# Late field pairs and seven weight tiles loaded in two parts: 112 rows in 14 groups from GpSimd's queue, 16 rows from ScalarE's

## The chip, the cores and the metric

The kernel runs on one core of a Trainium2 chip. The metric is the time of one execution in device microseconds. Before the change it is 756.43 us, the median of 4 runs (756.16 to 756.96).

The engines in what follows: PE (TensorE), DVE (VectorE), ACT (ScalarE), POOL (GpSimd) and SP (SyncE). Transfers between HBM and the on-chip memory are issued by an engine's queue and carried by 16 DMA engines.

## The reference: products of field pairs

For a batch of 1024, 32 fields of 128 numbers, and one 128 x 128 weight matrix for each of the 496 pairs of fields i < j:

```python
v_i = inputs[:, I_IDX, :]
v_j = inputs[:, J_IDX, :]
transformed = jnp.einsum('bpd,ped->bpe', v_i, W)
return transformed * v_j
```

All in float32. The output, 1024 x 496 x 128 numbers, is 260 MB; the inputs are 16.8 MB of fields and 32.5 MB of weights.

## The kernel before

**Data.** The host hands over the fields as `xt[d, field, batch]` and the weights as `wt[c, d, pair, e]`, eight pairs to a tile `c`, in the order of the work. On the chip d, later e, lies on the 128 partitions. One field is a tile of 128 x 1024 (512 KB, 4 KB in a row), a weight tile 128 x 8 x 128 (also 512 KB), an output buffer `ot` 128 x 4 x 1024 (2 MB: four pairs).

**Order.** `_pairs` (L31) lists the pairs with i from 30 down to 0 and j from i + 1 to 31. The main loop (L195) steps through u = 2 x pair + half; a half is 512 of the batch. The order of instructions is that of the program text (`manual_schedule`, L157), so each engine works through its list as written. `first(u)` (L161) starts a half, `second(u)` (L174) ends it three steps later (LAG).

**Work of a half.** The first 15 pairs use float32 matmuls (L168). All later ones split both sides in a high and a low part and use three fast matmuls: two at L171, ACT scales the sum in place (L172), a third is added at L180. DVE multiplies with field j into `ot` (L186). Then SP sends the buffer off, one transfer of 2 MB per four pairs (L193). The pool `o` has three buffers (L68): the fourth group can't be written before the first has gone out.

**Splits.** `split_w` (L95) makes the three parts of two pairs' weights: one instruction on ACT (L100), three on POOL (L101 to L103). `split_x` (L109) does it for half a field: ACT L115, POOL L116 and L117, and the third part on POOL (L121) or, for the first fields, on DVE (L214). The list `todo` (L129) holds them by the pair that needs them; the loop takes at most one of them per pair (L208 to L212), a weight chunk from five pairs ahead of its use on.

**Loads.** The first fields and weight tiles are loaded at the start. After that `load_x` (L73) loads field i - 7 at the first pair of row i (L199), and `load_w` (L88) loads weight tile c into one of three buffers (WB) at the pair that `w_at` (L148) names. Both are issued from ACT's queue, 128 rows at a time. Field 0 comes last, into a weight buffer (L204). POOL issues no transfer.

Of the kernel before, what the change touches and what calls it, by code (L numbers as in the profile page):

```python
# [7 lines left out]
F32 = mybir.dt.float32  # L8
# [3 lines left out]
P = 128  # L12
NF = 32
NQ = NF * (NF - 1) // 2
BT = 1024
HB = 512
WC = 2
WL = 8
# [7 lines left out]
WLEAD = 12  # L26
XAFTER = 54
XLEAD = 5


def _pairs():  # L31
# [5 lines left out]
def kernel(  # L37
# [22 lines left out]
    nc = tc.nc  # L60
# [3 lines left out]
    xpool = ctx.enter_context(tc.tile_pool(name="x", bufs=1))  # L64
# [6 lines left out]
    x_sb = {}  # L71

    def load_x(f, n=1, pieces=1, eng=None):  # L73

        if f == 0:

            t = rpool.tile([P, WL, P], F32, tag="w", name="x_0").rearrange("p q e -> p (q e)").unsqueeze(1)
        else:
            t = xpool.tile([P, n, BT], F32, tag=f"x{f}", name=f"x_{f}")
        s = BT // pieces  # L80
        for k in range(pieces):
            (eng or nc.sync).dma_start(out=t[:, :, k * s : (k + 1) * s], in_=xt[:, f : f + n, k * s : (k + 1) * s])
        for k in range(n):
            x_sb[f + k] = t[:, k, :]

    w_raw = {}

    def load_w(c, splits=(0, WL), eng=nc.scalar):  # L88
        w_raw[c] = rpool.tile([P, WL, P], F32, tag="w", name=f"w_{c}")
        for a, b in zip(splits, splits[1:]):  # L90
            eng.dma_start(out=w_raw[c][:, a:b, :], in_=wt[c, :, a:b, :])

# [30 lines left out]
    nq0 = NATIVE * (NATIVE + 1) // 2  # L123
# [11 lines left out]
    todo.sort(key=lambda t: t[1])  # L135

    load_w(0, (0, 1, WL), nc.sync)
    load_x(NF - 2, pieces=2, eng=nc.scalar)
    load_x(NF - 1, pieces=2, eng=nc.scalar)
    load_x(NF - 3)  # L140
    load_x(NF - 4)
    load_w(1, eng=nc.sync)
    for f in range(NF - 5, NF - 4 - XLEAD, -1):
        load_x(f)
    load_w(2, eng=nc.sync)


    w_at = {}  # L148
# [4 lines left out]
    x_at = XAFTER * WL - 11  # L153
    assert x_at not in w_at and len(w_at) == NQ // WL - WB


    ctx.enter_context(tc.manual_schedule())  # L157
    po, ots = {}, {}
# [2 lines left out]
    def first(u):  # L161
        q, h = divmod(u, 2)
        i, c = pairs[q][0], q // WC
        r = slice(q % WC * P, (q % WC + 1) * P)
        s = slice(h * HB, (h + 1) * HB)
        po[u] = ppool.tile([P, HB], F32, tag="po", name=f"po_{u}")
        if q < nq0:
            nc.tensor.matmul(po[u], w_raw[q // WL][:, q % WL, :], x_sb[i][:, s], start=True, stop=True)  # L168
        else:
            for t in (0, 1):  # L170
                nc.tensor.matmul(po[u], w_s[c][t][:, r], x_s[i][t][:, s], start=t == 0, stop=t == 1)  # L171
            nc.scalar.mul(po[u], po[u], 1.0 + EPS)  # L172

    def second(u):  # L174
        q, h = divmod(u, 2)
        i, j = pairs[q]
        r = slice(q % WC * P, (q % WC + 1) * P)
        s = slice(h * HB, (h + 1) * HB)
        if q >= nq0:
            nc.tensor.matmul(  # L180
                po[u], w_s[q // WC][2][:, r], x_s[i][2][:, s], start=False, stop=True, skip_group_check=True
            )
        g, k = divmod(q, OG)
        if k == 0 and h == 0:
            ots[g] = opool.tile([P, OG, BT], F32, tag="ot", name=f"ot_{g}")
        nc.vector.tensor_tensor(ots[g][:, k, s], po.pop(u), x_sb[j][:, s], ALU.mult)  # L186
        if q >= NQ - 2:
            nc.sync.dma_start(out=out[g, :, k, s], in_=ots[g][:, k, s])
        elif g == 0 or q >= NQ - OG:
            if h == 1:  # L190
                nc.sync.dma_start(out=out[g, :, k], in_=ots[g][:, k])
        elif k == OG - 1 and h == 1:
            nc.sync.dma_start(out=out[g], in_=ots[g])  # L193

    for u in range(2 * NQ + LAG):  # L195
        q = u // 2
        if u < 2 * NQ:
            i, j = pairs[q]
            if u % 2 == 0 and j == i + 1 and 0 < i - 2 - XLEAD:  # L199
                load_x(i - 2 - XLEAD, eng=nc.scalar)  # L200
            first(u)
            if u % 2 == 1 and q in w_at:
                load_w(w_at[q])
            if u == 2 * x_at + 1:  # L204
                load_x(0, eng=nc.scalar)
        if u >= LAG:
            second(u - LAG)
        if u % 2 == 1:  # L208
            ready = [t for t in todo if t[0] <= q]
            if ready:  # L210
                ready[0][2](u)
                todo.remove(ready[0])  # L212
        while later and later[0][0] <= u:
            nc.vector.tensor_tensor(*later.pop(0)[1:], ALU.subtract)  # L214
# [28 lines left out]
```

## Time and profile before

| | |
|---|---|
| median of 4 runs | 756.43 us |
| the profiled execution | 756.16 us, its span 754.3 us |
| busy: PE, DVE, ACT, POOL | 706.7, 624.4, 631.3, 596.5 us |
| moved by DMA | 310 MB in 33,039 packets, 411 GB/s over the span |
| read and written in HBM | 49.3 MB and 260.0 MB |
| loads: issue to landing | 10.6 us (weights from ACT), 11.2 us (fields from ACT), medians |

The span is the time from the first to the last instruction. Part 1 of the page gives each engine's busy time, part 2 the same in 40 slices, part 3 the queues (q1 carries SP's transfers, q10 ACT's, the two of kind "instruction" the engines' code), part 4 the chain of waits that ended last, part 5 the costliest groups of instructions, part 6 the transfers with the time from issue to landing. Matmuls overlap on PE, so the mean length of one is not their distance; that is read from the timeline.

### The profile page before, as it was taken

The page shows a single profiled execution, that of the slowest core. Times are in us where ns is not written, and L with a number is a line of the kernel's source. Part 1 is how long each engine was busy: PE and PEld are TensorE (multiplying, and loading weights), DVE is VectorE, ACT ScalarE, POOL GpSimd, SP SyncE. Part 2 cuts the span into 40 slices and gives each one's busy share as a digit, 9 for nine tenths or more (in the row PEclk, how much of TensorE's full clock was granted, in tenths as well). Part 3 has the DMA queues.
Part 4 walks back from the last instruction along what each step waited for, and adds up shares of the span by engine and source line. Part 5 has one row for each costly group of instructions (what it writes and reads, how often), then busy time and mean ns, then how long its engine had stood idle before and what let it go on. Part 6 is the DMA issues. An engine that isn't in the chain of part 4 may idle for free.

```text
span 754.3 us, 11212 instructions
## 1 busy us (share of the span) xinstructions
PE 706.7 (94%) x2946; PEld 548.0 (73%) x2946; DVE 624.4 (83%) x1012; ACT 631.3 (84%) x1256; POOL 596.5 (79%) x863
## 2 busy tenths in 40 slices
PE   7989999999999999999999999999999999999993
PEld 3567777767777777777777778778787777777872
DVE  4889998888787788888788898888888888898884
ACT  1388988888888888898888889898898998888992
POOL 0988999888888987978879697888887878696660
PEclk9999999999999999999999999999999999999997
DMA  9999999999999999999999999999999999999997
GB/s 352 427 425 428 428 424 428 405 421 395 421 426 414 416 413 409 427 391 428 410 408 425 409 404 421 428 409 407 424 406 412 409 407 407 421 381 429 427 416 301
DMA packets 33039, 310.06 MB, mean 411 GB/s; under 512 B 3664, under 2 KB 3792, under 8 KB 17360
## 3 DMA queue, kind: packets, MB, share of 16 engines
q1 hardware_dynamic: 20448, 264.77, 84.1%
q10 hardware_dynamic: 12528, 44.57, 15.3%
q8 instruction: 24, 0.39, 0.2%
q14 instruction: 39, 0.32, 0.1%
HBM read 49.28 MB, written 260.05 MB: 410 GB/s over the span
## 4 chain that ended last, share of the span: by engine, by line
DMA 43%; PE 28%; DVE 20%; POOL 5%; issue 2%; ACT 0%; DVEq 0%; ACTq 0%; SPq 0%; POOLq 0%
DMA out_dram<-ot 41%; DVE ot L186 19%; PE po L171 19%; PE po L180 9%; DMA x<-in_xt_dram 2%; POOL xl L116 2%; POOL xd L121 1%; DVE xd L214 1%; POOL xl L117 1%; POOL wl L101 1%; POOL wd L103 0%; POOL wd L102 0%; ACT xh L115 0%; DVEq L186 0%; ACT po L172 0%
## 5 line engine op out<-in xcount | busy, mean ns | idle before, releaser
L186 DVE TENSOR_TENSOR ot<-po,x 128x512 f32<-128x512 f32 x992 | 611.1, 683 | 115.2 <-DMA out_dram<-ot 51.4
L172 ACT ACTIVATE po<-po 128x512 f32<-128x512 f32 x962 | 547.5, 584 | 88.0 <-PE po L171 42.8
L171 PE MATMUL po<-xh,wh 128*128 128x512 f32 x962 | 382.1, 397 | 18.5 <-DVE ot L186 17.4
L171 PE MATMUL po<-xl,wl 128*128 128x512 f32 x962 | 377.2, 392 | 9.2 <-POOL wl L101 9.0
L180 PE MATMUL po<-xd,wd 128*128 128x512 f32 x962 | 376.4, 392 | 3.2 <-DVE xd L214 2.7
L171 PEld LDWEIGHTS po<-xh,wh 128*128 128x128 f32 x962 | 180.9, 188 | 80.4 <-DVE ot L186 42.8
L101 POOL TENSOR_TENSOR wl<-w,wh 128x256 fp32r<-128x256 f32 x241 | 180.7, 750 | 71.1 <-ACT wh L100 67.6
L171 PEld LDWEIGHTS po<-xl,wl 128*128 128x128 f32 x962 | 181.0, 188 | 49.2 <-POOL wl L101 14.5
L180 PEld LDWEIGHTS po<-xd,wd 128*128 128x128 f32 x962 | 181.0, 188 | 44.1 <-ACT po L172 4.2
L103 POOL TENSOR_TENSOR wd<-wl,wd 128x256 fp32r<-128x256 f32 x241 | 180.3, 748 | 20.1
L102 POOL TENSOR_SCALAR wd<-wh 128x256 fp32r<-128x256 f32 x241 | 99.5, 413 | 20.3
L100 ACT ACTIVATE wh<-w 128x256 fp32r<-128x256 f32 x241 | 99.5, 413 | 5.6 <-DMA w<-in_wt_dram 4.0
L116 POOL TENSOR_TENSOR xl<-x,xh 128x512 fp32r<-128x512 f32 x52 | 68.8, 1324 | 20.2 <-ACT xh L115 19.8
L121 POOL TENSOR_TENSOR xd<-xh,xl 128x512 fp32r<-128x512 f32 x32 | 41.4, 1292 | 2.7
L115 ACT ACTIVATE xh<-x 128x512 fp32r<-128x512 f32 x52 | 32.6, 631 | 12.3 <-DMA x<-in_xt_dram 12.2
L117 POOL TENSOR_SCALAR xl<-xl 128x512 fp32r<-128x512 f32 x52 | 33.1, 637 | 4.6
L168 PE MATMUL po<-x,w 128*128 128x512 f32 x60 | 28.1, 631 | 4.2 <-DMA x<-in_xt_dram 4.2
L168 PEld LDWEIGHTS po<-x,w 128*128 128x128 f32 x60 | 11.6, 200 | 19.8 <-issue 12.1
L214 DVE TENSOR_TENSOR xd<-xh,xl 128x512 fp32r<-128x512 f32 x20 | 16.1, 807 | 3.9 <-POOL xl L117 3.9
L115 ACT ACT_TABLE_LOAD x1 | 1.3, 1283 | 4.1 <-DMA w<-in_wt_dram 4.1
L230 POOL MEMSET const-float32-0.0<- 128x1 f32 x1 | 0.1, 99 | 0.2 <-issue 0.2
L230 POOL MEMSET const-bfloat16-1.0<- 128x1 bf16 x1 | 0.1, 103 | 0.0
(2 smaller groups left out, 0.2 us busy)
## 6 DMA issues: line engine op xcount, KB each, us to landing
out_dram<-ot SPq DMA_DIRECT2D x122, 2048.0 KB, 12.5
w<-in_wt_dram ACTq DMA_DIRECT2D x59, 512.0 KB, 10.6
x<-in_xt_dram ACTq DMA_DIRECT2D x24, 512.0 KB, 11.2
x<-in_xt_dram SPq DMA_DIRECT2D x6, 512.0 KB, 8.6
out_dram<-ot SPq DMA_DIRECT2D x6, 512.0 KB, 9.9
x<-in_xt_dram ACTq DMA_DIRECT2D x4, 256.0 KB, 5.6
w<-in_wt_dram SPq DMA_DIRECT2D x2, 512.0 KB, 8.2
out_dram<-ot SPq DMA_DIRECT2D x4, 256.0 KB, 8.9
```

Of the source, the lines that this page charges most:

```text
L100: nc.scalar.mul(h, raw, 1.0 - 2.0**-13)
L101: nc.gpsimd.tensor_tensor(l, raw, h.bitcast(F32), ALU.subtract)
L102: nc.gpsimd.tensor_scalar(d, h.bitcast(F32), EPS, 1.0, ALU.mult, ALU.mult)
L103: nc.gpsimd.tensor_tensor(d, l.bitcast(F32), d.bitcast(F32), ALU.subtract)
L116: nc.gpsimd.tensor_tensor(l, x_sb[f][:, s], h.bitcast(F32), ALU.subtract)
L117: nc.gpsimd.tensor_scalar(l, l.bitcast(F32), 1.0 / EPS, 1.0, ALU.mult, ALU.mult)
L121: nc.gpsimd.tensor_tensor(d, h.bitcast(F32), l.bitcast(F32), ALU.subtract)
L168: nc.tensor.matmul(po[u], w_raw[q // WL][:, q % WL, :], x_sb[i][:, s], start=True, stop=True)
L171: nc.tensor.matmul(po[u], w_s[c][t][:, r], x_s[i][t][:, s], start=t == 0, stop=t == 1)
L172: nc.scalar.mul(po[u], po[u], 1.0 + EPS)
L180: nc.tensor.matmul(po[u], w_s[q // WC][2][:, r], x_s[i][2][:, s], start=False, stop=True, skip_group_check=True)
L186: nc.vector.tensor_tensor(ots[g][:, k, s], po.pop(u), x_sb[j][:, s], ALU.mult)
```

## The change

Fields 14 to 1 are loaded in twos, (13, 14) to (1, 2), 8 KB in a row, at the pairs (i, i + 8) for i = 17, 15, ... 5. These seven loads and those of weight tiles 45, 47, 49, 51, 54, 57 and 59 go through `load_apart`: rows 0 to 111 are issued by POOL, rows 112 to 127 by ACT. For the first part the source is written as 14 groups of 8 rows with a step of 14 rows between the rows of a group, and the host puts the rows of these fields and tiles in that order, so that they arrive where they did.

`move_on(k)` issues a transfer of 2 k rows of 64 bytes in k groups from POOL, into a tile that nothing reads: k = 5 at the first split pair, k = 2 three pairs after each load that went apart, k = 13 after the last. 5 + 14 x 14 + 13 x 2 + 13 is 240. The older fields down to 15, field 0 and the other weight tiles are loaded as before. The pairs' order, the splits and the outputs stay as they are, and the instructions other than transfers keep their order on every engine. `dynamic_dma_scratch_size` goes from 256 to 2048.

```diff
--- before.py
+++ after.py
@@ -28,6 +28,18 @@
 XLEAD = 5
 
 
+NE = 14
+ROWS = 8 * NE
+XAPART = 14
+XSTEP, XPOS = 4, 8
+WAPART = (45, 47, 49, 51, 54, 57, 59)
+BACK = 3
 def _pairs():
 
     return [(i, j) for i in range(NF - 2, -1, -1) for j in range(i + 1, NF)]
@@ -85,8 +97,28 @@
 
     w_raw = {}
 
+    mark = xpool.tile([32, 16], F32, tag="mark", name="mark")
+    def move_on(k):
+        nc.gpsimd.dma_start(out=mark[: 2 * k], in_=xt[: 2 * k, 0, :16].rearrange("(b a) n -> a b n", a=k))
+    def load_apart(dst, src):
+        nc.gpsimd.dma_start(out=dst[:ROWS], in_=src[:ROWS].rearrange("(b a) m n -> a b m n", a=NE))
+        nc.scalar.dma_start(out=dst[ROWS:], in_=src[ROWS:])
+    def load_x_apart(f):
+        t = xpool.tile([P, 2, BT], F32, tag=f"x{f}", name=f"x_{f}")
+        load_apart(t, xt[:, f : f + 2, :])
+        for k in range(2):
+            x_sb[f + k] = t[:, k, :]
     def load_w(c, splits=(0, WL), eng=nc.scalar):
         w_raw[c] = rpool.tile([P, WL, P], F32, tag="w", name=f"w_{c}")
+        if c in WAPART:
+            load_apart(w_raw[c], wt[c])
+            return
         for a, b in zip(splits, splits[1:]):
             eng.dma_start(out=w_raw[c][:, a:b, :], in_=wt[c, :, a:b, :])
 
@@ -152,6 +184,9 @@
         w_at[max(c * WL - 3 * WC - 5 - early, free)] = c
     x_at = XAFTER * WL - 11
     assert x_at not in w_at and len(w_at) == NQ // WL - WB
+    w_q = {c: q for q, c in w_at.items()}
+    back = []
 
 
     ctx.enter_context(tc.manual_schedule())
@@ -196,11 +231,21 @@
         q = u // 2
         if u < 2 * NQ:
             i, j = pairs[q]
-            if u % 2 == 0 and j == i + 1 and 0 < i - 2 - XLEAD:
+            if u % 2 == 0 and j == i + 1 and XAPART < i - 2 - XLEAD:
                 load_x(i - 2 - XLEAD, eng=nc.scalar)
             first(u)
+            if u == 2 * nq0:
+                move_on(5)
+            f = i - XSTEP
+            if u % 2 == 0 and 0 < f < XAPART and f % 2 == 1 and j == i + XPOS:
+                load_x_apart(f)
+                back.append(q + BACK)
             if u % 2 == 1 and q in w_at:
                 load_w(w_at[q])
+                if w_at[q] in WAPART:
+                    back.append(q + BACK)
+            if u % 2 == 0 and q in back:
+                move_on(16 - NE if q < w_q[WAPART[-1]] else 13)
             if u == 2 * x_at + 1:
                 load_x(0, eng=nc.scalar)
         if u >= LAG:
@@ -225,9 +270,13 @@
     x = _np.asarray(inputs["r_inputs"])
     w = _np.asarray(inputs["L0_rec_W"])
     xt = _np.ascontiguousarray(x.transpose(2, 1, 0))
+    late = xt[:ROWS, 1 : XAPART + 1].reshape(NE, 8, XAPART, BT)
+    xt[:ROWS, 1 : XAPART + 1] = late.transpose(1, 0, 2, 3).reshape(ROWS, XAPART, BT).copy()
     wt = _np.ascontiguousarray(w[perm].reshape(NQ // WL, WL, P, P).transpose(0, 3, 1, 2))
-
-    nc = _bacc.Bacc("TRN2", target_bir_lowering=False, num_devices=1, dynamic_dma_scratch_size=256)
+    for c in WAPART:
+        wt[c, :ROWS] = wt[c, :ROWS].reshape(NE, 8, WL, P).transpose(1, 0, 2, 3).reshape(ROWS, WL, P).copy()
+    nc = _bacc.Bacc("TRN2", target_bir_lowering=False, num_devices=1, dynamic_dma_scratch_size=2048)
     arrays, args = {}, []
     for name, a in (("xt", xt), ("wt", wt)):
         arrays[f"in_{name}_dram"] = a
```

## The prediction

> **What bounds the kernel now.** I read the page first: part 1 (engines), part 2 (the DMA rows), part 3 (queues), then the chain in one stretch, then the windows.
>
> ```profile
> PE 706.7 (94%) x2946; PEld 548.0 (73%) x2946; DVE 624.4 (83%) x1012; ACT 631.3 (84%) x1256; POOL 596.5 (79%) x863
> ...
> DMA  9999999999999999999999999999999999999997
> ...
> q1 hardware_dynamic: 20448, 264.77, 84.1%
> q10 hardware_dynamic: 12528, 44.57, 15.3%
> q8 instruction: 24, 0.39, 0.2%
> q14 instruction: 39, 0.32, 0.1%
> ...
> out_dram<-ot SPq DMA_DIRECT2D x122, 2048.0 KB, 12.5
> ```
>
> No compute engine is full in every slice, the DMA row is. Parts 3 and 6: 310 MB pass, nearly all of it output, and an output takes 12.5 us to land. The two instruction rows are small as a share of 16 engines, but not as a share of one: q8's 24 packets of 16 KB last 23.8 us in the packet records (0.2% of 16 x 754.3 = 24.1), q14's 39 packets 12.1 us.
>
> The chain between 577 and 604 us shows what DMA holds up:
>
> ```profile
> 566.29 13.23 DMA out_dram<-ot
> ...
> 579.65 4.89 DVE ot L186 x8
> ...
> 584.55 11.65 DMA out_dram<-ot
> ...
> 596.33 4.89 DVE ot L186 x8
> ```
>
> DVE fills an output buffer (4.89 us), the buffer goes out (11.65 to 13.23 us), and DVE may refill it only when its *last* byte is out. With three buffers one such cycle of some 17.6 us carries three groups of four pairs, 5.87 us each. So the slowest part of each transfer counts.
>
> Which part is slow, the landing records tell. Each transfer raises its semaphore 16 times, once per DMA engine. Median us from issue to the 7th, 14th, 15th and 16th of these, over the 2 MB outputs issued in each stretch:
>
> ```
> stretch      7th    14th   15th   16th
> 20 to 60    10.56  11.43  11.68  12.61
> 150 to 250   8.75  10.59  11.57  13.03
> 350 to 450   7.62   8.93  11.42  12.71
> 550 to 650   7.11   8.10   9.51  12.35
> ```
>
> Fourteen engines finish together; one is 2 to 4 us behind them and a second 1 to 2.5. They have the same rows of every transfer as the others, so they do something besides: an extra 24 and 12 us of instruction packets on one engine each would do it (inference: the records name no engine; but no two packets of q8 overlap, as on one engine). Once the lag is as long as the buffers allow, the fourteen idle. The windows show that point:
>
> ```profile
> core 0: us, PE busy (x) PEld busy (x) DVE busy (x) ACT busy (x) POOL busy (x), PEclk, DMA share, GB/s
> 50.00:100.00 50.00, 46.27 (x191) 36.63 (x192) 48.21 (x75) 42.61 (x87) 44.31 (x62) 0.97 1.01 427
> ...
> 150.00:700.00 550.00, 526.75 (x2248) 416.47 (x2247) 460.95 (x752) 487.27 (x971) 453.89 (x662) 1.00 1.00 413
> ```
>
> While the lag builds up: 427 GB/s. After that: 413. If 427 is what the fourteen can do, they lose 550 x (1 - 413/427) = 18.0 us there. Nineteen of q8's packets, 19.2 us, lie in the same stretch: two ways to one size.
>
> **The change, part by part.** The order of all compute instructions on PE, DVE, ACT and POOL stays; only DMA issues move, so the sum has few terms. Profiled execution: 756.16 us (span 754.3 and 1.9 around it), 0.3 below the median 756.43.
>
> *Rows per engine.* Now every load gives each engine 8 of 128 rows. After it, for seven double fields and seven weight tiles, 112 rows go in 14 groups of 8, and 16 rows go one to each of 16 engines. Fourteen engines get 9 rows, two get 1. Packet medians: 4 KB 159 ns, 8 KB 309 ns, 16 KB 611 ns. A double field was 16 x 159 = 2.54 us per engine; it becomes 9 x 309 = 2.78 or 0.31. A weight tile was 8 x 159 = 1.27; it becomes 1.43 or 0.16. Over 7 + 7 loads the fourteen gain 7 x 0.24 + 7 x 0.16 = **2.8 us**, and the two lose 7 x 2.23 + 7 x 1.11 = 23.4. Relative to the fourteen the two win 26.2 us, more than either laggard's fetches in that stretch (19.2 us, and 12.1 x 550/754 = 9).
>
> *Spacing.* The loads stand at pairs 98, 127, 160, 197, 238, 283, 332 (fields) and 343 to 455 (weights), by the output issues 167 to 688 us. Between two field loads 40 to 75 us pass, in which the slow engine loses about 18/550 of the time, 1.3 to 2.5 us; a field load returns 2.47, a weight load 1.27 every 23 to 46 us. So the lag should fall to 1 or 2 us and stay there. That takes the 18.0 us away, **-18.0**, and leaves the fourteen's **+2.8**.
>
> *Tail.* The last output's increments: 14th at 4.55 us, 15th 5.61, 16th 7.92. The span ends with the 16th; 3.4 us are to be had. After the last moved load some lag grows again: **-2.0** (0 to -3.4).
>
> *What is late next.* In the late stage PE is close behind. Its matmul starts there stand 0.228 us apart, 24 per group: 5.47 us; the groups from 527 to 677 us took 5.78, and at 427 GB/s with the ninth row they would take 5.60. PE cannot run at 98% through waits for DVE and POOL, so I give back a third of that stage's share (500 to 700 us: 411 GB/s, 7.5 us): **+2.5** (0 to 7.5).
>
> *GpSimd's queue.* 14 loads and 15 small transfers are issued by POOL, which issues none now, so the trace has no price. Nearest rows: ACT's issue of the same loads, 0.33 us, and POOL's longest own row, L116's 1.32. 29 of them are 10 to 38 us of POOL's time; POOL is idle 157.8. Behind each issue stand the weight splits L101 to L103, 1.9 us per chunk, for which PE waits already (14 times, 14.5 us). A chunk is put in 5 pairs (7.3 us) before its use, which covers an issue of the bounded size; the field splits, which take up that lead, come at the start of a row of pairs, and the field loads at its eighth pair. Without any cover 14 x 1.32 = 18.5 us would show; I take **+1.5** (0 to 18.5), near the low end, as most of it lies in idle time. The loads wait for nothing on POOL: a field's buffer is its own, and a weight buffer's last reader is POOL itself. The waits of the small transfers are for the one before, 20 us and more earlier: nothing. ACT issues 14 instructions for 21: 7 x 0.33 = 2.3 us less, hidden, since ACT is idle 16%. The double fields are loaded 22 pairs and more (30 us) ahead of their first split against 10 to 16 us to land: hidden.
>
> Sum: 756.16 - 18.0 + 2.8 - 2.0 + 2.5 + 1.5 = **743.0 us**.
>
> [...] No run here names the engines.
>
> **Rivals.**
> - *The two left out are not the laggards.* For it: no row says which engines lag, and the 14 groups fall on some fixed choice. Against: two lag and two are left out. The laggards then get 9 rows for 8 and stay the bound: 756.2 + 2.8 + 1.5 = 760.5 (757.5 to 765). It decides as soon as the heavier laggard is among the fourteen.
> - *No uneven share:* if GpSimd's queue spreads 112 rows over all 16 engines, each has 7 + 1 = 8, as now. For it: the before has no such transfer. Time 756.2 + 0 to 1.5: 757.
> - *One laggard is left out, the heavier:* the other's 12.1 us of fetches (9 in the stretch) and 2.8 more stay: of 18.0 some 6 come back, 752.
>
> **Chances.** Forecast 0.72 (736 to 751, by the bounds above; 429 GB/s, which is 16 engines at 611 ns per 16 KB, gives the low end), wrong engines 0.12, even share 0.08, one laggard 0.05, POOL's issues above their cover 0.03 (over 757). The range takes the forecast's cases, the one laggard's and the even share: 735 to 758. Within 0.2% (1.5 us, about what a measurement can tell from no change) lie the even share and little else: 0.08. Faster: 0.72 and most of the one laggard, 0.76. Slower: 0.16.
>
> **What would show it.** Right: GB/s between 150 and 700 us at 423 or more, DVE's wait for out_dram far below its 51.4 us, the 16th increment within 2 us of the 14th, outputs landing in 11 us or less, a third data queue of some 1,600 larger packets. Wrong engines: the 16th later than now, GB/s at 412 or less. Even share: the table of increments unchanged. POOL too dear: PE waiting for wl L101 well above its 9.0 and 14.5 us. The forecast fails on size if PE's late stage gives back more than a third.

## The result and the profile after

The changed kernel takes **754.59 us**, the median of 53 runs (749.45 to 763.39), beside 756.56 us of the kernel before (73 runs, 755.93 to 757.17). The ratio is 0.9977, with a 95% interval of 0.9967 to 0.9986: some 2 us faster, where 13 were forecast. The second thing to see is the width. The kernel before stays within 1.2 us, the changed one varies by 14. The profiled execution took 753.4 us, its span 751.6.

From the page of the changed kernel (engines; DMA row; queues; costliest groups with busy time, mean ns and idle time before; transfers with us to landing):

```profile
PE 700.0 (93%) x2946; PEld 552.2 (73%) x2946; DVE 659.9 (88%) x1012; ACT 626.8 (83%) x1256; POOL 613.0 (82%) x892
...
DMA  9999999999999999999999999999999999999998
...
q1 hardware_dynamic: 20448, 264.77, 84.0%
q10 hardware_dynamic: 9952, 34.94, 11.8%
q0 software_dynamic: 2496, 9.64, 3.8%
q8 instruction: 24, 0.39, 0.2%
q14 instruction: 39, 0.32, 0.1%
...
L104 POOL DMA_DIRECT2D mark<-in_xt_dram x15 | 9.6, 642 | 0.1
...
L107 POOL DMA_DIRECT2D w<-in_wt_dram x7 | 4.4, 626 | 0.0
...
out_dram<-ot SPq DMA_DIRECT2D x122, 2048.0 KB, 11.4
...
x<-in_xt_dram POOLq DMA_DIRECT2D x7, 896.0 KB, 14.4
```

GpSimd's loads are the new queue q0, and one issue costs POOL 0.62 to 0.64 us. The outputs land in 11.4 us for 12.5. But the shares of part 3 add up to 99.9% of the span, as they did before (99.7%): the DMA engines are as full as they were. (Packet records overlap now and then, up to 21 on 16 engines, so the sum alone could hide some idle time; a count of the packets that run at once, further down, finds little.)

The waits of the kernel before (engine, line, what it waited for: us in total, times, longest; PEld is the weight load of PE):

```profile
DVE ot L186 <- DMA out_dram<-ot: 51.4, 51, 2.1
...
PEld po L171 <- POOL wl L101: 14.5, 14, 1.9
...
PE po L171 <- POOL wl L101: 9.0, 11, 1.6
...
ACT wh L100 <- DMA w<-in_wt_dram: 4.0, 3, 1.5
```

and those of the changed kernel:

```profile
DVE ot L221 <- DMA out_dram<-ot: 37.2, 29, 3.7
PEld po L206 <- POOL wl L133: 28.8, 23, 2.2
...
PE po L206 <- POOL wl L133: 19.7, 20, 1.8
...
ACT wh L132 <- DMA w<-in_wt_dram: 5.5, 3, 2.7
```

DVE's wait for the outputs fell from 51.4 to 37.2 us, and PE's waits for POOL rose from 9.0 and 14.5 to 19.7 and 28.8. A wait has changed its place more than it has gone.

The windows of the changed kernel:

```profile
core 0: us, PE busy (x) PEld busy (x) DVE busy (x) ACT busy (x) POOL busy (x), PEclk, DMA share, GB/s
50.00:100.00 50.00, 46.53 (x199) 36.25 (x197) 49.12 (x75) 43.74 (x90) 46.15 (x63) 1.00 1.00 423
650.00:700.00 50.00, 45.43 (x191) 36.10 (x190) 43.13 (x65) 39.71 (x82) 38.30 (x58) 0.97 0.97 390
150.00:700.00 550.00, 518.76 (x2232) 417.80 (x2231) 483.18 (x746) 480.31 (x964) 469.01 (x687) 0.99 1.00 414
```

Between 150 and 700 us 414 GB/s pass, against 413 before and the 427 that I forecast. Yet most of the lag is gone. Medians over that stretch, us from an output's issue to its 7th, 14th, 15th and 16th increment:

```
kernel                        7th    14th    15th    16th   mean of 16th - 14th
before                        7.51   8.99   10.74   12.59   3.37
changed                       9.06  10.32   10.76   11.45   1.19
changed, other run            9.23  10.48   10.91   11.70   1.11
share left even (even16)      7.74   8.92    9.89   12.26   3.39
other first transfer (shift8) 7.73   8.62    9.40   12.38   3.67
```

So the change does what it says, and that is worth little. More than half of the fall comes from the fourteen: their last increment comes 1.33 us later than before (10.32 for 8.99), while the last of all sixteen, which DVE waits for, comes 1.14 us earlier. Where the gain is lost, the times at which DVE starts a pair show, as the difference to the kernel before in us (one profile each; kernels in the next section):

```
pair                            272    336    432    448    495
double_act: ACT's queue only   -5.5    1.1    0.9    0.9    0.9
even16: share even             -4.1    0.4    3.3    3.3    8.7
changed                       -10.3   -6.3   -4.4   -0.6   -0.4
no57: tile 57 by ACT           -8.3   -5.8   -5.3   -3.3   -4.8
x_late: fields only            -6.0   -4.5   -5.2   -4.7   -5.0
```

Up to pair 272 some 5 us are only put off: four of the fields that the kernel before had loaded by then (4 x 1.27 = 5.1 us per engine) come later, and `double_act` shows them paid back by pair 336. Against `double_act` the changed kernel is 7.4 us ahead at pair 336 and 1.3 at pair 495. The weight tiles, which go apart from pair 343 on, lie in between. (Single profiles of one program differ by several us at such a place, so the times of whole runs below have to confirm this.) Its span is 2.7 us shorter than before: 0.4 from the body, and 2.2 from the last output's 16th increment (5.70 us after issue for 7.92).

### The profile page after: what moved, and what is told of

The parts are those of the page before. It is cut to its first block, busy times and chain, and to the rows that moved or that the text cites. A ratio compares the mean times of both kernels' runs of the same rounds, so it can differ in the third digit from the quotient of the medians.

```text
span 751.6 us, 11269 instructions
## 1 busy us (share of the span) xinstructions
PE 700.0 (93%) x2946; PEld 552.2 (73%) x2946; DVE 659.9 (88%) x1012; ACT 626.8 (83%) x1256; POOL 613.0 (82%) x892
## 4 chain that ended last, share of the span: by engine, by line
PE 47%; DMA 25%; DVE 16%; POOL 9%; issue 1%; ACT 0%; DVEq 0%; POOLq 0%; ACTq 0%
PE po L206 29%; DMA out_dram<-ot 23%; DVE ot L221 15%; PE po L215 14%; PE po L203 4%; POOL wl L133 2%; POOL xl L148 2%; POOL xd L153 2%; POOL wd L135 2%; DMA w<-in_wt_dram 1%; POOL xl L149 1%; DVE xd L259 1%; POOL wd L134 1%; DMA x<-in_xt_dram 1%; ACT po L207 0%
## 5 line engine op out<-in xcount | busy, mean ns | idle before, releaser
L221 DVE TENSOR_TENSOR ot<-po,x 128x512 f32<-128x512 f32 x992 | 642.8, 687 | 80.4 <-DMA out_dram<-ot 37.2
L206 PE MATMUL po<-xl,wl 128*128 128x512 f32 x962 | 378.7, 394 | 19.9 <-POOL wl L133 19.7
L206 PE MATMUL po<-xh,wh 128*128 128x512 f32 x962 | 378.0, 393 | 11.3 <-DVE ot L221 11.3
L206 PEld LDWEIGHTS po<-xl,wl 128*128 128x128 f32 x962 | 181.4, 189 | 66.6 <-POOL wl L133 28.8
L135 POOL TENSOR_TENSOR wd<-wl,wd 128x256 fp32r<-128x256 f32 x241 | 178.5, 741 | 20.1
L134 POOL TENSOR_SCALAR wd<-wh 128x256 fp32r<-128x256 f32 x241 | 98.9, 411 | 20.5
L148 POOL TENSOR_TENSOR xl<-x,xh 128x512 fp32r<-128x512 f32 x52 | 68.9, 1325 | 19.7 <-ACT xh L147 19.4
L203 PEld LDWEIGHTS po<-x,w 128*128 128x128 f32 x60 | 12.1, 207 | 21.2 <-issue 13.6
L259 DVE TENSOR_TENSOR xd<-xh,xl 128x512 fp32r<-128x512 f32 x20 | 20.0, 1001 | 2.7 <-POOL xl L149 2.0
L104 POOL DMA_DIRECT2D mark<-in_xt_dram x15 | 9.6, 642 | 0.1
L107 POOL DMA_DIRECT2D w<-in_wt_dram x7 | 4.4, 626 | 0.0
## 6 DMA issues: line engine op xcount, KB each, us to landing
out_dram<-ot SPq DMA_DIRECT2D x122, 2048.0 KB, 11.4
```

Source lines behind the costliest of these rows:

```text
L134: nc.gpsimd.tensor_scalar(d, h.bitcast(F32), EPS, 1.0, ALU.mult, ALU.mult)
L135: nc.gpsimd.tensor_tensor(d, l.bitcast(F32), d.bitcast(F32), ALU.subtract)
L148: nc.gpsimd.tensor_tensor(l, x_sb[f][:, s], h.bitcast(F32), ALU.subtract)
```

## The experiments

The theories when they began: **relief** (the two left-out engines are the laggards, the lag held the fourteen idle, and something else now takes the gain), **wrong engines**, **no uneven share**, and **POOL** (its issues are the next bound). The recorded expectations name their theories by letters, each explained where it first stands. Ratios are to the kernel before, with 95% intervals; edits are to the changed kernel unless said otherwise, and `...` marks lines left out.

**again**: the changed kernel unedited.

> The changed kernel once more, for a second profile and the width of its times. Theory S (the relief works, and what it frees is lost again in stalls at the late loads, each followed by a halved PE clock for some 3.4 us): times spread over 750 to 760 us, the 16th increment of the outputs within 1.5 us of the 14th, one to five stretches of halved clock in mid-run at places that differ from the first profile. Rival Q (GpSimd's queue itself is dear): the same time at every run, no new clock drops. Rival L (the lagging engines were never the bound): lag gone, time within 0.3% of before in every run.

755.47 us (747.09 to 760.22, 12 runs), ratio 0.996 [0.9933, 0.9986]. The profiled execution took 747.09, 8 us less than the median of the same program. In mid-run it has two stretches of halved clock, at other places than the first profile, as theory S expected; the lag is gone (1.11 us) and the times spread widely, against rivals Q and L.

**even16**: the same queues and sizes, without the uneven share.

```diff
-        nc.gpsimd.dma_start(out=dst[:ROWS], in_=src[:ROWS].rearrange("(b a) m n -> a b m n", a=NE))
+        nc.gpsimd.dma_start(out=dst[:ROWS], in_=src[:ROWS])
...
-                move_on(5)
+                move_on(6)
...
-                move_on(16 - NE if q < w_q[WAPART[-1]] else 13)
+                move_on(16 - NE if q < w_q[WAPART[-1]] else 16)
```

(The host leaves the rows in their order, and the first and last small transfer have other sizes.)

> The same 14 loads through GpSimd's queue with the same small transfers, but the 112 rows plain, for 7 rows on each of 16 engines: no uneven share. Theory S: the lag of before is back (16th 3 us and more behind the 14th) and holds the time at 756 to 760 us, narrow. Rival Q: the queue's cost without its gain, 765 us and more. Rival L: as the changed kernel, 752 to 757, since the share is of no matter.

761.71 us (760.47 to 761.84), ratio 1.0062 [1.005, 1.0074]. The lag is back at 3.39 us. So the uneven share is real, and worth 761.71 - 754.59 = 7.1 us; what else the change brings costs 5.2, which no theory had (S up to 760, Q from 765 on). The last step of it is one wait. ACT's timeline in `even16`:

```profile
689.10 0.42 ACT L132 ACTIVATE wh<-w 128x256 fp32r<-128x256 f32 x1 [5.99 <-DMA w<-in_wt_dram]
```

and the same place in the changed kernel:

```profile
681.85 0.42 ACT L132 ACTIVATE wh<-w 128x256 fp32r<-128x256 f32 x1 [2.68 <-DMA w<-in_wt_dram]
```

The first split of tile 57 waits for the tile. In `even16` GpSimd issues its part 2.5 us behind ACT's (676.94 and 674.42 us), and it lands 12.0 us later; in the changed kernel it is 1.0 us behind and lands after 10.3. The long wait in `even16` goes with 6.8 us of halved clock, the one in the changed kernel with none.

**shift8**: the first small transfer of 13 groups for 5 and the last of 5 for 13, meant to leave other engines out of the loads between them.

```diff
-                move_on(5)
+                move_on(13)
...
-                move_on(16 - NE if q < w_q[WAPART[-1]] else 13)
+                move_on(16 - NE if q < w_q[WAPART[-1]] else 5)
```

> [...] Theory S: the laggards then carry 9 rows for 8: the 16th increment further back than before, 759 to 765 us. Rival Q and rival L: no difference from the changed kernel, 750 to 760.

765.81 us (765.41 to 766.63), ratio 1.012 [1.0105, 1.0134], with the lag at 3.67 us. That is above theory S's 759 to 765. It does matter which engines are left out, by 11.2 us, and the changed kernel leaves out the one that lags most. Rivals Q and L, which expected no difference, fall.

**floor**: the kernel before, writing out only two of each four pairs.

```diff
-            nc.sync.dma_start(out=out[g], in_=ots[g])
+            nc.sync.dma_start(out=out[g, :, :2], in_=ots[g][:, :2])
```

> The kernel before with half of each 2 MB output transfer left out (two of four pairs are not written): the time of everything but DMA. Theory S: 715 to 735 us, below what the fourteen engines need (some 735), so that compute has room on average but not much. Rival L: 745 and more, compute is the bound. Rival Q says nothing here.

727.85 us (2 runs), ratio 0.962 [0.9603, 0.9636]. That is the compute chain by itself. Its window, 150 to 700 us:

```profile
150.00:700.00 550.00, 530.49 (x2319) 433.81 (x2318) 526.56 (x776) 497.65 (x999) 464.88 (x682) 1.00 0.66 241
```

At 241 GB/s PE is busy 530.49 of 550 us and DVE 526.56. Compute needs about 728 us when outputs hold it up no more; what the DMA engines need comes below.

**double_act**: the kernel before with the fields loaded in twos at the new places, all by ACT, on all engines alike; as an edit of the changed kernel:

```diff
-WAPART = (45, 47, 49, 51, 54, 57, 59)
+WAPART = ()
...
-        load_apart(t, xt[:, f : f + 2, :])
+        nc.scalar.dma_start(out=t, in_=xt[:, f : f + 2, :])
```

(The small transfers and the host's order of the rows go too.)

> The kernel before with only the fields 14 to 1 in twos at the changed places, all 128 rows from ACT's queue; no GpSimd transfer, weights as before. It asks where the 5 us come from that the even share lost against before (761.7 to 756.6). Theory G (packets on GpSimd's queue occupy an engine longer: 3.8% of the span for 9.64 MB in the changed kernel, where ACT's rate of 15.3% for 44.57 MB would give 3.3%, some 4 us per engine): 756 to 757.5, no loss. Rival B (the 1 MB bursts stall the pipeline): 759 to 762, with three or more clock drops at the field loads.

756.76 us, ratio 1.0003 [0.9995, 1.0012]. Size and place of the field loads are worth nothing by themselves.

**single**: the uneven share for 14 single fields at the places of before, so 21 loads and 22 small transfers.

```diff
-        t = xpool.tile([P, 2, BT], F32, tag=f"x{f}", name=f"x_{f}")
-        load_apart(t, xt[:, f : f + 2, :])
-        for k in range(2):
+        t = xpool.tile([P, 1, BT], F32, tag=f"x{f}", name=f"x_{f}")
+        load_apart(t, xt[:, f : f + 1, :])
+        for k in range(1):
...
```

> The uneven share kept, but the 14 fields one by one, 4 KB in a row, at the places that before loads them; weights as in the changed kernel; 21 loads and 22 small transfers from POOL. Rival B: bursts of half the size and an earlier relief give 744 to 750. Theory G: the queue's cost goes by bytes and packets, and grows if anything: 753 to 758.

762.91 us (758.4 to 764.52), ratio 1.008 [1.0059, 1.0102]. Its waits:

```profile
PEld po L206 <- POOL wl L133: 42.5, 24, 3.3
PE po L206 <- POOL wl L133: 32.5, 20, 2.9
...
ACT wh L132 <- DMA w<-in_wt_dram: 8.0, 3, 5.8
DVE ot L221 <- DMA out_dram<-ot: 7.9, 9, 1.5
```

The lag is down to 0.78 us and DVE hardly waits for outputs, and still it is slower than before, and than both theories had it (758 at most): PE waits for POOL, whose field loads and splits come together at the start of a row of pairs. By these waits POOL bounds here; no run lightens POOL in this version.

**only_x**: the field pairs apart, all weight tiles by ACT. **only_w**: the reverse.

```diff
-WAPART = (45, 47, 49, 51, 54, 57, 59)
+WAPART = ()
```

> The changed kernel with the seven double fields alone; the weights all from ACT. Relief lasts until about 515 us, after it the lag grows back by some 3% of the time to its limit. Theory S (relief real, lost again in part at the loads): 752 to 757, and the pairs from 352 on at the pace of before. If the weights' part is the one that costs, 748 to 752.

748.95 us (745.26 to 756.95, 10 runs: seven up to 749.4, three from 755.4), ratio 0.9895 [0.9872, 0.9919]. Its profiled execution took 756.64 us, so its trace is not read for the gain.

```diff
-XAPART = 14
+XAPART = 0
```

> The changed kernel with the seven weight tiles alone; the fields one by one from ACT as before. Relief 7 x 1.27 us between 527 and 690 us, about twice what the lag grows in that time: no bursts of 1 MB. Theory S: the stretch to pair 336 as before, then 3 to 5 us won and 2 at the end: 750 to 753. Theory G takes about 2 of it: 752 to 755. If the relief were worth nothing so late: 756 to 758.

757.73 us (754.48 to 764.22, 12 runs), ratio 1.0025 [1.0004, 1.0047]. The fields bring all of the gain, and the weight tiles take most of it away again. For `only_w` theories S and G had a gain (755 at most); there is none.

**no57**: tile 57 back to ACT. **no57_late**: that, and the first split of tiles 55 to 57 two pairs later.

```diff
-WAPART = (45, 47, 49, 51, 54, 57, 59)
+WAPART = (45, 47, 49, 51, 54, 59)
```

and for the later split:

```diff
-        todo.append(((c - 3) * WC + 1, max(c * WC, nq0), lambda u, c=c: split_w(c, u)))
+        late = 2 if c * WC % WL == 0 and XAFTER < c * WC // WL <= XAFTER + WB else 0
+        todo.append(((c - 3) * WC + 1 + late, max(c * WC, nq0), lambda u, c=c: split_w(c, u)))
```

> The changed kernel with weight tile 57 back on ACT's queue, whole; all else as changed. Tile 57 is loaded only six pairs (some 8.5 us) ahead of its first split, and its GpSimd part lands 10 us and more after the issue; ACT waited for it 2.7 us in the changed kernel and 6.0 with the even share. Theory W (this late tile, not the path as such, is the weights' loss): 749 to 752, the wait at the tile's split 1.5 us or less. Theory G (GpSimd's packets cost engine time): 754, as one load of fourteen matters little.

> As the kernel without tile 57, and the first split of tiles 55, 56 and 57 may start two pairs later, so that ACT, which works in order, does not stand before a tile that has not landed. Theory W: 746 to 750, ACT's wait for weights under 1.5 us in all, no halved clock near 665 us. If these waits cost nothing (ACT catches up): as the kernel without tile 57, within 1 us.

749.43 us, ratio 0.992 [0.9889, 0.9951], and 749.53 us, 0.9906 [0.9891, 0.9921]. One of seven tiles costs (0.9977 - 0.9920) x 756.6 = 4.3 us (by the intervals 0.5 to 7). Of that the profiles show 1.7 as a shorter wait for the tile itself, 0.99 us in `no57`:

```profile
677.50 0.42 ACT L132 ACTIVATE wh<-w 128x256 fp32r<-128x256 f32 x1 [0.99 <-DMA w<-in_wt_dram]
```

Where the rest lies is not shown. The later split cuts ACT's waits for weights from 2.6 to 1.0 us in all, and no gain can be told.

**x_late**: only the fields apart, and the later split. **x_w4**: fields and tiles 45, 47, 49, 51.

> The double fields alone (the weights from ACT), with the same later first split of tiles 55 to 57. The double fields alone took 749 in median, and there the late stage ran at the pace of before, bound by the lag. Theory W: little to gain where the lag is the bound: 747 to 750. If ACT's waits set the late stage: 744 to 747.

> The double fields and the weight tiles 45, 47, 49 and 51 from GpSimd; 54, 57 and 59 from ACT. Theory W: relief without a late tile: 747 to 751, the best of the changed kernel's kind. Theory G: between the double fields alone (749) and the changed kernel (754.6): 751 to 754.

748.5 us, ratio 0.9894 [0.9874, 0.9913], and 751.3 us, 0.9921 [0.9898, 0.9945]. With the lag already down, more relief by weight tiles brings nothing; 751.3 lies between the ranges of theories W and G and decides neither.

**x_late_sh**: x_late with six more fields' third parts on DVE for POOL. **before_sh** and **floor_sh**: the same line in the kernel before, and in `floor` (which leaves out the same writes).

```diff
-SHARED = 10
+SHARED = 16
```

> The double fields alone with the later first splits (748.5 us), and in it the third part of the splits of fields 15 to 10 on DVE instead of POOL (SHARED 16 for 10): 12 instructions of 1.29 us off POOL, 12 of 0.8 to 1.0 us onto DVE. Theory P (with the lag gone POOL's weight splits are the next bound): 743 to 746. Theory D (DMA bursts and halved clocks alone hold it): 748 to 750, or later, as DVE has more to do.

> The kernel before with the same six fields' third part on DVE. Both theories: within 0.2% of before (755.5 to 758), as the lagging engines set its time; a gain here would say that POOL bounds the kernel before as well.

> The kernel before with half of each 2 MB output transfer left out (two of four pairs are not written), with the same six fields' third part on DVE. Theory P: the floor of 727.9 us falls by 4 to 10 us, and PE's wait for POOL with it. Theory D: 727 to 729.

748.56 us (745.54 to 752.93), ratio 0.9899 [0.987, 0.9928]; 757.24 us, 1.0008 [0.9999, 1.0016]; 718.51 us, 0.9497 [0.9483, 0.9511]. Less work for POOL takes 9.3 us from the compute chain alone and nothing from the whole kernel. The theory that POOL is the next bound of the fields-only kernel falls; in `single`, with 43 issues on POOL, the waits speak for it.

**before_light**: the kernel before without the low and third parts and ACT's scaling (all three matmuls read the high parts; the corrections are left out). **no57_light**: the same on `no57`. **no57_light2**: on `no57`, with POOL's weight splits kept but unread, so that POOL's loads keep their times.

```diff
-                nc.tensor.matmul(po[u], w_s[c][t][:, r], x_s[i][t][:, s], start=t == 0, stop=t == 1)
-            nc.scalar.mul(po[u], po[u], 1.0 + EPS)
+                nc.tensor.matmul(po[u], w_s[c][0][:, r], x_s[i][0][:, s], start=t == 0, stop=t == 1)
...
```

> The kernel before with light compute: the low and third parts of both splits and ACT's scaling are left out, all three matmuls use the high parts, so the output is another one; transfers, PE's instructions and DVE's are those of before. With the lagging engines as the bound (theory S): 750 to 757, nearly as before, and the 16th increment 3 to 5 us behind the 14th. If compute had a part in it: below 748.

> The changed kernel without tile 57 (749.4 us), with the same work left out. Coupling (PE, POOL and ACT lose what the relief frees): 736 to 742, some 13 us below the light kernel before, and narrow. Relief over-sized: 745 to 749, 7 us below it, as with the full work.

> As the light kernel with the relief (all three matmuls use the high parts, ACT's scaling is left out, the output is another one), but POOL's split instructions stay, read by nobody, so that POOL issues its loads in step with the work. To be held against the light kernel before, 747.5 us. Coupling: 734 to 740, at least 8 us below it. Relief over-sized: 741 to 745, 3 to 6 us below it.

747.49 us (746.79 to 748.4), ratio 0.9883 [0.9866, 0.9899]; 768.85 us, 1.016 [1.0135, 1.0185]; 747.19 us (741.67 to 750.88), 0.9878 [0.9819, 0.9937]. `no57_light` says nothing on the question: without the splits nothing held POOL back, all seven field loads were issued in the first 48 us, and pair 16 came 38 us late. The other two do. The windows of `before_light` and of `no57_light2`, 150 to 700 us:

```profile
150.00:700.00 550.00, 533.82 (x2274) 420.43 (x2273) 461.38 (x758) 97.54 (x223) 0.00 (x0) 1.00 1.01 418
```

```profile
150.00:700.00 550.00, 526.33 (x2265) 421.90 (x2264) 463.23 (x756) 96.27 (x220) 469.30 (x692) 1.00 1.01 420
```

With little compute beside it the full lag (3.3 us in `before_light`) costs little: 747.5 with it, 747.2 without. Had the compute chain taken the gain of the relief, `no57_light2` should stand well below `before_light`; both theories had it lower (745 at most), but its interval is wide, and some 5 us can't be excluded. `before_light` by itself lies under 748, where its expectation gave compute a part. The two differ in one thing more: POOL still does its splits in `no57_light2` (469 us) and nothing in `before_light`. And 418 to 420 GB/s is what passes in both.

## Why the prediction was right in sign and wrong in size

**That the left-out pair holds the laggard, and that the share is uneven: right.** The trace of before named neither; `shift8` (11.2 us) and `even16` (7.1 us) show both, as far as the one that lags most goes. The landings of the changed kernel show the two engines apart: in each of its 14 loads by GpSimd two of the 16 increments come 0.8 to 3.1 us ahead of the third, where in the kernel before no load has more than 0.53 us between its second and third. That an increment is one engine's, as the prediction read it, fits the packet records of before: just after 717.5 us, where q1 runs alone, an output ends in 16 packets of 4 bytes, and 15 of the next output's 16 come 4.86 us behind them, the time of eight packets of 16 KB (0.61 us each). Up to its last load `shift8` differs from the changed kernel by nothing but the groups of the first small transfer (13 for 5), so which engines a load leaves out goes with what GpSimd issued before; in what order the engines take the groups, no run shows. Whether a second laggard is left out too is not shown. The 15th increment does come to the 14th (0.44 us behind it for 1.75), but in `double_act`, with every load even, it is 0.68 behind, and in `shift8` 0.79: the second laggard that the prediction counted on is not steady. What makes engines lag, the instruction fetches or something else, no run shows.

**The term -18.0: the step that failed.** "While the lag builds up: 427 GB/s. After that: 413. If 427 is what the fourteen can do, they lose 550 x (1 - 413/427) = 18.0 us there." The lag went, and the rate came to 414. In the fastest profile of a kernel that computes everything (`x_late_sh`, span 744.3 us) it is this:

```profile
150.00:700.00 550.00, 526.33 (x2269) 423.81 (x2269) 484.76 (x769) 489.80 (x979) 454.53 (x671) 1.00 1.01 421
```

So 427 was a rate of the stretch from 50 to 100 us, and no kernel here kept it. And the loss was not idle time. Part 3 of before adds up to 99.7%, which I read only for the instruction rows; and in the packet records of before, 16 packets or more run at once for 540.4 of the 550 us, and 8 or fewer for 2.3. Fourteen engines that idle for 18.0 us would leave at most a few packets running for as long. That this figure agreed with the time of q8's packets in the stretch was a coincidence (18 of them start there, 18.3 us; the prediction counted one more).

Taking each packet at the median of its size, an engine needs 730 us in every kernel of this table. How much longer the packet records take stands in the column "packets over their median", in us per engine. "Fewer than 16" is the time between 150 and 700 us with fewer than 16 packets running, "lacking" what was lacking to 16 then, in us per engine:

```
kernel           span    packets over their median   fewer than 16   lacking
before           754.3   21.8                         9.6            2.4
changed          751.6   21.3                        10.8            3.3
again            745.3   16.8                         7.5            1.6
even16           760.1   26.7                        18.1            5.1
shift8           764.8   30.3                        24.3            5.1
x_late_sh        744.3   15.2                         2.6            0.2
before_light     745.7   15.3                        16.0            1.3
no57_light2      743.1   13.8                         6.8            0.9
```

The 18.0 us of idle time were 2.4. Of the 20.5 us between `x_late_sh` and `shift8` some 15 are longer packets and 5 lacking ones. I had counted as idle time what are longer packets, and as if the lag alone stood between the kernel and full rate. The lag alone does not set their length either: the changed kernel has 21.3 us without it, `before_light` 15.3 with it. The term's size, had the change kept its gain, is 7.1 us by `even16`, 7.8 by `only_x` against `double_act`.

What holds the kernel near 745 us then is argued, not shown. Compute alone takes 728 us (`floor`). Packets take 730 us and at least some 14 more in these profiles; that is no floor that was measured by itself, and one run of `no57_light2` has a span of 739.9. What stands above goes when the lag is removed (`x_late`, 748.5) or when compute is light (`before_light`, 747.5), but not twice (`no57_light2`, 747.2). Light compute goes with shorter packets (15.3 us over their medians for 21.8), so `before_light` does not test the compute chain alone. A limit behind the engines, of the memory for one, was not tested either.

**GpSimd's queue, +1.5: right in its price, wrong in its place.** The issue costs 0.62 to 0.64 us, 29 of them 18.4 us, inside the bounds that I gave, and with 15 of them the kernel is at its fastest (`only_x`). What costs is the landing: I ruled out a late load for the fields (rightly, 13 to 16 us against 30) and did not ask it of the weight tiles. ACT wants tile 57 some 9 us after its issue. In `no57`, all 128 rows by ACT, it lands after 10.1 us, 1.0 too late; behind POOL's queue it is 2.7 us late in the changed kernel and 6.0 in `even16`. By `no57` its price is 4.3 us, which no term of the sum had. The mark that I set for "POOL too dear", PE's wait above 9.0 and 14.5 us, came true in the changed kernel (19.7 and 28.8) but misled: `x_late_sh` cuts it to 13.6 and is no faster than `x_late`.

**Smaller terms.** Tail, -2.0: measured 2.2, but by luck as far as the runs tell. In `even16` and `shift8`, with the lag in place, the last increment also comes 5.0 us after the issue. Ninth row, +2.8: not seen by itself. `double_act` bears out that the moved loads cost nothing. PE's late stage, +2.5: not seen by itself; the stretch from 650 to 700 us fell to 390 GB/s, where tile 57's wait and a halved clock (below) lie.

**The rivals.** Wrong engines was priced at 760.5 (757.5 to 765): `shift8`, 765.8. No uneven share at 757: `even16`, 761.7. Both named the mechanism and were 5 us too low; in `even16` the step of some 5 us near the end is tile 57's, which the forecast lacked too, and `shift8` waits 7.1 us at the same place. One laggard left out, priced at 752: the increments do not decide it, since the 15th falls without an uneven share as well (`double_act`).

**Open.** Why packets last longer than their median in some executions and not in others; and with it the width of 749 to 763 us, which the mean clock doesn't explain (0.989 in the run of 763.39 us, 0.988 in that of 749.50). No experiment here sets the packets' length by itself.

**The best version** is the change without its weight tiles: 748.5 to 749 us (`only_x`, `x_late`, `x_late_sh`), 1.05% below the kernel before and 0.8% below the changed one.

## What to carry to other kernels

Before the time lost to a slow resource is booked as a gain, add up the busy shares of that resource (here 99.7%) and run or estimate the other bound by itself: where two bounds lie within a few per cent, removing one gives back only the part that the other leaves. A load that moves to a busier queue is priced by its landing against its first use, not by its issue alone, and each load has its own lead. And of a relief only so much pays as the lag needs: seven field pairs brought all of it, seven weight tiles more took most of it back. And a wait at the end of a slow part is no proof that the rest stood idle: count what was running meanwhile.

## What the runs showed of the hardware

**The clock fell after some short stalls, here of 1.46 to 1.82 us.** PE in the changed kernel (start, us, instruction, idle time before):

```profile
525.74 0.50 PE L206 MATMUL po<-xh,wh 128*128 128x512 f32 x1 [1.82 <-DVE ot L221]
526.07 0.39 PE L206 MATMUL po<-xl,wl 128*128 128x512 f32 x1
526.30 0.40 PE L215 MATMUL po<-xd,wd 128*128 128x512 f32 x1
526.53 0.59 PE L206 MATMUL po<-xh,wh 128*128 128x512 f32 x1
526.93 0.63 PE L206 MATMUL po<-xl,wl 128*128 128x512 f32 x1
```

After 1.82 us without a matmul the granted clock is halved from 526.6 us for 3.4 us (PEclk 0.50):

```profile
526.60:530.00 3.40, 3.40 (x10) 2.63 (x9) 3.36 (x6) 1.65 (x3) 0.21 (x1) 0.50 0.97 399
```

Matmuls start 0.43 us apart for 0.23. At half the rate PE loses some 1.7 us in 3.4; by this estimate a wait that is 1 us longer can cost it 2.7. The changed kernel has two such falls in its body (the other after 1.80 us), the kernel before one, after 1.46 us, `single` seven, one of them twice as long. It isn't strict: 1.82 us at 448 us passed without one, and so did two stalls of 2.21 us in `single`.

**DMA engines lagged without any transfer of GpSimd, and not always the same number.** By the medians, the kernel before has its 15th increment 1.75 us and its 16th 3.6 behind the 14th. In `double_act` it is one engine (0.68 and 4.3). In `before_sh` three fall back: its 14th is 2.3 us behind its 12th, and its 16th only 1.5 behind the 14th, at the time of before. So a distance between two increments is a poor measure of the lag by itself. No run here names the engines.

**Packets stretched where engines idled.** In `floor`, with the engines idle some 225 us each, ACT's loads take 55 us per engine more than their packets' medians; in the kernel before it is 6. What stretches them is not shown.
